# The head of a scan kernel: sums first, convolution by lines with two tiles in turn, first delta inside SBUF

## Chip, core and metric

The kernel runs on one NeuronCore of one Trainium2 chip. The metric is the device time of one execution in microseconds (us). TensorE is called PE, VectorE DVE, ScalarE ACT, GpSimd POOL, and SyncE SP; SP here issues most of the DMAs.

## What is computed

The input x is (4, 64, 64, 96) in f32: four images ("batches") of 4096 positions with 96 channels. Layer 0 is a binary hybrid of convolution and selective scan; layer 1 is an attention without softmax and a quantised feed-forward. Only layer 0 of the first batch is touched by the change:

```python
# x: (4, 64, 64, 96); Dn = 192, N = 16, R = 6, K = 4 directions, L = 4096
xz = bilinear(gn(x), W_in, s_in, b_in)          # sign(x - group mean) @ sign(W - mean).T, 384 wide
xp, z = split(xz, 2)
t = sign(xp + move0)
t = conv3x3(t, scale * sign(conv_W)) + conv_b   # 192 -> 192
t = prelu(t) + rp_b1 + xp
u = silu(t)                                     # (B, 192, 64, 64)
xs = [u by rows, u by columns, both reversed]   # K = 4
dts, Bs, Cs = split(bilinear(xs, Wl, sl, bl))   # R + 2 N rows ("rows" below)
delta = softplus(bilinear(dts, Wd, sd, bd) + dt_bias)
for each direction k, channel d, state n:       # along L
    h[l] = exp(delta[l] * A[n]) * h[l-1] + delta[l] * u[l] * B[n, l]
    y[l] += h[l] * C[n, l]
y = layernorm(y + D * u) * silu(z)              # then sign(...) into W_out
x = x + bilinear(y, W_out, s_out, b_out)
# ... layer 1: x + attention(ln(x)), x + ffn(ln(x))
```

## The kernel before

The scan is cut into 1536 pieces of 128 partitions by 1024 positions (32 channels times 4 states). Each takes an Exp on ACT ("decay"), a product delta·u·B on POOL ("inject"), a scan on DVE, a product with C on POOL or DVE, and a sum over states on PE. The pieces of one batch overlap with the other batches' remaining stages; what stands ahead of the first piece, for batch 0 alone, is called the head (`alone` is true there). `run` advances two generators in turn, the preparation of weights (`weights`) and the stages of batch 0 (`prologue`), until the rows of the first direction are there.

The loads of the constants inside `weights` (sbR: scale and bias of the rows; anm: the state matrix A):

```python
nc.gpsimd.memset(sbR, 0.0)
for k in range(NK):
    o, r0 = k % 2, 64 * (k // 2)
    nc.scalar.dma_start(sbR[r0 : r0 + 32, o, 0:1], a["sl_bc"][0:32, k : k + 1])
    nc.scalar.dma_start(sbR[r0 : r0 + 32, o, 1:2], a["bl_bc"][:, 32 * k : 32 * k + 32].rearrange("o p -> p o"))
    nc.scalar.dma_start(sbR[r0 + 32 : r0 + 32 + NR, o, :], a["sl_dt"][k])
for g in range(NG):
    src = a["al"][32 * (g % 4) : 32 * (g % 4) + 32, g // 4].rearrange("d k (q j) -> j d (k q)", j=4)
    for j in range(4):
        nc.sync.dma_start(anm[j::4, g, :], src[j])
for t in gTs + [wdz]:
    nc.gpsimd.memset(t.bitcast(F32), 0.0)

# ... [cut: mean and sign of W_in, its transposes]
# ... [cut: weight transposes through two PSUM banks with tags y0, y1 (`transposed`), reductions, casts]
```

The sums over x and the first sign of batch 0 (`c.later.store` puts a DMA into a list that `tick` issues on SP later; `bank(name, j)` gives one of the PSUM banks y0, y1):

```python
csum = bank("csum", 0)[0:1, 0 : 4 * DM]
for i in range(0, NT, 4):
    nc.tensor.matmul(
        csum, c.ones1, xts[i // 8][:, i % 8 : i % 8 + 4, :].rearrange("p i e -> p (i e)"),
        start=(i == 0), stop=(i == NT - 4),
    )
    if i % 8 == 4:
        yield
row = f32("csr")[0:1, 0 : 4 * DM]
nc.scalar.copy(row, csum)
# ... [cut: two small matmuls turn the row and add the groups]
negm = f32("negm")[0:96, 0:1]
nc.scalar.mul(negm, gsum, -1.0 / (3 * L))

def xfin(q, ps):
    cols = slice(512 * q, 512 * q + 512)
    nc.scalar.activation(xsT[:, cols], ps, AF.Sign, bias=negm, saturate=False)
    t = f32(f"xb{q}")[0:96]
    nc.scalar.activation(t, ps, AF.Identity, bias=c.bo)
    c.later.store(c.xbd[b][:, cols], t)

# ... [cut: transposes of x feed xfin, 8 tiles]
```

The projection of one part (h: half of the channels, q: eighth of the image) and the convolution:

```python
two = [c.p.dA.tile([128, CH], F32, name=f"cv{i}_{b}", tag="dA") for i in range(2)] if alone else None

def project(h, q):

    cols = slice(512 * q, 512 * q + 512)
    if alone:
        px, pz = two[1][:, 0:512], two[1][0:96, 512:CH]
    else:
        px, pz = bank(f"ix{h}{q}", 0), bank(f"iz{h}{q}", 1)[0:96]
    nc.tensor.matmul(px, c.winB if h else c.winT[:, 0:128], xsT[:, cols], start=True, stop=True)
    nc.tensor.matmul(
        pz, c.winT[:, DN + 96 * h : DN + 96 * h + 96], xsT[:, cols], start=True, stop=True
    )
    yield
    for rows, back in ((slice(0, 64), 0), (slice(64, 128), 1)) if h else ((slice(0, 128), 0),):
        nc.scalar.activation(
            tpad[h][rows, 1 + 8 * q : 9 + 8 * q, 1 - back : 1 - back + IW],
            px[rows].rearrange("p (h w) -> p h w", w=IW), AF.Sign,
            scale=c.pvx[rows, h, S_X : S_X + 1], bias=c.sbx[rows, h : h + 1], saturate=False,
        )
    sz = c.p.h.tile([128, CH], F32, name=f"sz{h}{q}_{b}", tag="h") if alone else f32(f"sz{h}{q}")
    sz = sz[0:96, 0:256].bitcast(BF16)
    nc.scalar.activation(
        sz, pz, AF.Sign, scale=pv[:, h, S_Z : S_Z + 1], bias=pv[:, h, B_Z : B_Z + 1]
    )
    c.later.store(c.szd[b][h][:, cols], sz)
# ... [cut: the first four projections ahead]
parts = [(h, q) for h in range(2) for q in range(NQ8)]
# ... [cut]
def by_columns(h, q, u):

    if q % 4 == 0:
        uts[h] = utp.tile([96, IW, 32], F32, name=f"ut{h}{q}_{b}", tag="ut")
    ut, at = uts[h], 8 * (q % 4)
    dst, src = ut[:, :, at : at + 8], u.rearrange("p (h w) -> p w h", w=IW)
    (nc.gpsimd.tensor_copy if alone else nc.scalar.copy)(dst, src)
    if q % 4 == 3:
        rows = slice(8 * q - 24, 8 * q + 8)
        c.later.store(c.utd[b][h].rearrange("p (w h) -> p w h", h=IH)[:, :, rows], ut, after=1)

# ... [cut: sign(h, q, pz) makes sg on ACT and stores it to xg in three pieces]
for n, part in enumerate(parts + [None]):
    if part:
        h, q = part
        nm = f"{h}{q}"
        at = 512 * (n % 2)
        ps = (two[0][:, at : at + 512] if alone else bank("cv" + nm, 0))[0:96]
    for s in range(4 if alone else 5):
        if part:
            per = 4 if alone else 3
            for tp, w, dy, dx in taps[per * s : per * s + per]:
                nc.tensor.matmul(
                    ps, w[:, 96 * h : 96 * h + 96], tp[:, 8 * q + dy : 8 * q + dy + 8, dx : dx + IW],
                    start=(w is taps[0][1]), stop=(w is taps[-1][1]),
                )
        if alone and ahead:
            if s % 2 == 0:
                next(ahead[0])
            else:
                next(ahead.pop(0), None)
        if prev:                    # [abridged to the case of alone]
            if s == 0:
                c.vec.scalar_tensor_tensor(pz, pz, pv[:, ph, S_X : S_X + 1], v, ALU.mult, ALU.add)
                c.vec.scalar_tensor_tensor(pz, r, c.oma[:, one(ph)], pz, ALU.mult, ALU.add)
            elif s == 1:
                sign(ph, pq, pz)
                nc.scalar.activation(e, pz, AF.Exp, scale=-1.0)
            elif s == 2:
                nc.scalar.activation(e, e, AF.Ln, bias=1.0)
                nc.scalar.activation(e, e, AF.Exp, scale=-1.0)
            elif s == 3:
                c.vec.tensor_tensor(u, pz, e, ALU.mult)
                c.later.store(c.ud[b][ph][:, 512 * pq : 512 * pq + 512], u)
                by_columns(ph, pq, u)
    if part:
        v, r = f32("v" + nm)[0:96], f32("r" + nm)[0:96]
        if alone:
            nc.vector.tensor_scalar(v, ps, c.acs[:, one(h)], c.acb[:, one(h)], ALU.mult, ALU.add)
        nc.scalar.activation(r, ps, AF.Relu, scale=c.csc[:, one(h)], bias=c.cbias[:, one(h)])
        pz = bank("cz" + nm, n % 2 if alone else 1)[0:96]
        nc.tensor.matmul(
            pz, c.winT[:, 96 * h : 96 * h + 96], xsT[:, 512 * q : 512 * q + 512], start=True, stop=True
        )
# ... [cut]
```

Then the rows: xr is turned from xg by PE and copied by ACT, the sums acc are scaled into tbc (B and C) and signed into sgn (dts):

```python
for o in (1, 0):
    xr = rw.tile([128, 96, 64], BF16, name=f"xr{o}_{b}", tag="xr")
    # ... [cut]
        if prev:
            nc.scalar.copy(prev[0], prev[1])
            prev = None
    # ... [cut]
                nc.scalar.activation(tbg[:, :, dv], sv, AF.Identity, scale=sc[0], bias=sc[1])
                nc.scalar.activation(sgg[:, :, dv], sv, AF.Sign, scale=sc[0], bias=sc[1], saturate=False)
# ... [cut]
```

Last, the first three parts of delta (`prepare`, ending in stores to dld in HBM), and the loop over pieces:

```python
def run(self, back):
    c, lanes, n = self.c, [], len(self.pieces)

    w = [c.p.w.tile([128, CH], F32, name=f"w_s{x}", tag="w") for x in range(8)]
    ps = [c.p.dA.tile([128, CH], F32, name=f"dA_s{x}", tag="dA") for x in range(2)]
    for x in range(3):
        half = slice(512 * (x % 2), 512 * (x % 2) + 512)
        lanes.append(
            self.prepare((
                w[x].rearrange("p (t l) -> p t l", t=2), w[3 + x // 2][:, half], w[5 + x // 2], ps[x // 2][:, half],
            ))
        )
    interleave(lanes)
    c.nc.scalar.activation(c.anm, c.anm, AF.Exp)
    c.nc.vector.tensor_scalar(c.anm, c.anm, -1.0, None, ALU.mult)
    for q in range(NQ):
        self.load_bc(0, self.bt, 0, 0, 0, q)
        self.load_bc(1, self.ct, 0, 0, 0, q)
    while lanes:
        interleave(lanes)
        c.later.tick()
    c.later.flush()
    self.load_dl(0)
    for m in (1, 2):
        self.load_dl(m)

    u = c.p.pu.tile([128, CH], F32, name="pu_s", tag="pu")
    for _ in self.prepare((w[7].rearrange("p (t l) -> p t l", t=2), w[4][:, 512:CH], u, ps[1][:, 512:CH])):
        pass
    self.decay(0)
    for i in range(AHEAD):
        self.inject(i)
    for i in range(n):
        self.at = i
        self.loads(i)
        # ... [cut: sums, carry, decay, reduce, inject, late product, scan of piece i]
```

Of the kernel before, what the change touches and what calls it, by code (L numbers as in the profile page):

```python
# [11 lines left out]
F32 = mybir.dt.float32  # L12
# [13 lines left out]
CH = 1024  # L26
# [27 lines left out]
def hybrid_kernel(ctx: ExitStack, tc: tile.TileContext, a: dict, out: bass.AP):  # L54
# [108 lines left out]
    def weights():  # L163
# [97 lines left out]
        for k in range(NK):  # L261
            o, r0 = k % 2, 64 * (k // 2)
            nc.scalar.dma_start(sbR[r0 : r0 + 32, o, 0:1], a["sl_bc"][0:32, k : k + 1])
            nc.scalar.dma_start(sbR[r0 : r0 + 32, o, 1:2], a["bl_bc"][:, 32 * k : 32 * k + 32].rearrange("o p -> p o"))
            nc.scalar.dma_start(sbR[r0 + 32 : r0 + 32 + NR, o, :], a["sl_dt"][k])
        for g in range(NG):
            src = a["al"][32 * (g % 4) : 32 * (g % 4) + 32, g // 4].rearrange("d k (q j) -> j d (k q)", j=4)
            for j in range(4):
                nc.sync.dma_start(anm[j::4, g, :], src[j])
        for t in gTs + [wdz]:  # L270
            nc.gpsimd.memset(t.bitcast(F32), 0.0)

# [113 lines left out]
        for name, dst in (("w1", w1q), ("w2", w2q), ("b1", b1q), ("b2", b2q)):  # L386
            q = dst if dst.dtype == F8 else temp(name + "q", list(dst.shape), F8)
            nc.vector.tensor_copy(q, small[name], saturate=False)
            if q is not dst:
                nc.vector.tensor_copy(dst, q)  # L390

# [58 lines left out]
def run(c):  # L450
# [6 lines left out]
    while (0, 1) not in c.ready:  # L457
        interleave(lanes)
        c.later.tick()
    scans = Scans(c)  # L460
# [39 lines left out]
def prologue(c, b, xts=None):  # L500
# [11 lines left out]
    with tc.tile_pool(name=f"xg_{b}", bufs=1) as xgp:  # L512
# [3 lines left out]
        with tc.tile_pool(name=f"cv_{b}", bufs=1) as cvp:  # L516
# [40 lines left out]
            def xfin(q, ps):  # L557
# [3 lines left out]
                nc.scalar.activation(t, ps, AF.Identity, bias=c.bo)  # L561
                c.later.store(c.xbd[b][:, cols], t)

            last = None
# [13 lines left out]
            two = [c.p.dA.tile([128, CH], F32, name=f"cv{i}_{b}", tag="dA") for i in range(2)] if alone else None  # L578

            def project(h, q):  # L580

                cols = slice(512 * q, 512 * q + 512)
                if alone:
                    px, pz = two[1][:, 0:512], two[1][0:96, 512:CH]
# [13 lines left out]
                sz = c.p.h.tile([128, CH], F32, name=f"sz{h}{q}_{b}", tag="h") if alone else f32(f"sz{h}{q}")  # L598
                sz = sz[0:96, 0:256].bitcast(BF16)
# [3 lines left out]
                c.later.store(c.szd[b][h][:, cols], sz)  # L603
# [16 lines left out]
            parts = [(h, q) for h in range(2) for q in range(NQ8)]  # L620
            taps = [(tpad[0], c.cwA[:, 3 * dy + dx], dy, dx) for dy in range(3) for dx in range(3)]
# [6 lines left out]
            def by_columns(h, q, u):  # L628

                if q % 4 == 0:  # L630
                    uts[h] = utp.tile([96, IW, 32], F32, name=f"ut{h}{q}_{b}", tag="ut")
                ut, at = uts[h], 8 * (q % 4)
                dst, src = ut[:, :, at : at + 8], u.rearrange("p (h w) -> p w h", w=IW)
                (nc.gpsimd.tensor_copy if alone else nc.scalar.copy)(dst, src)
                if q % 4 == 3:
                    rows = slice(8 * q - 24, 8 * q + 8)
# [12 lines left out]
            for n, part in enumerate(parts + [None]):  # L649
                if part:  # L650
                    h, q = part
                    nm = f"{h}{q}"
                    at = 512 * (n % 2)
                    ps = (two[0][:, at : at + 512] if alone else bank("cv" + nm, 0))[0:96]
                for s in range(4 if alone else 5):
# [7 lines left out]
                    if alone and ahead:  # L663
                        if s % 2 == 0:
                            next(ahead[0])
                        else:
# [53 lines left out]
        with tc.tile_pool(name=f"rw_{b}", bufs=1) as rw:  # L720

# [6 lines left out]
            for o in (1, 0):  # L728
                xr = rw.tile([128, 96, 64], BF16, name=f"xr{o}_{b}", tag="xr")
# [8 lines left out]
                for n in range(13):  # L738
                    if prev:
                        nc.scalar.copy(prev[0], prev[1])  # L740
# [17 lines left out]
                for gh in range(2):  # L758
                    groups = slice(32 * gh, 32 * gh + 32)
                    prev = None  # L760
                    for n in range(5):
                        if prev is not None:
# [3 lines left out]
                            nc.scalar.activation(tbg[:, :, dv], sv, AF.Identity, scale=sc[0], bias=sc[1])  # L766
# [429 lines left out]
class Scans:  # L1196
# [232 lines left out]

    def run(self, back):  # L1430
        c, lanes, n = self.c, [], len(self.pieces)

        w = [c.p.w.tile([128, CH], F32, name=f"w_s{x}", tag="w") for x in range(8)]
        ps = [c.p.dA.tile([128, CH], F32, name=f"dA_s{x}", tag="dA") for x in range(2)]
        for x in range(3):
            half = slice(512 * (x % 2), 512 * (x % 2) + 512)
            lanes.append(
                self.prepare((
# [133 lines left out]
```

## Time and profile before

| what | value |
| --- | --- |
| time, median of 3 runs | 5511.64 us (5508.68 to 5516.53) |
| span of the profiled execution | 5504.2 us |
| granted TensorE clock, mean | 0.717 |
| first sum over x on PE (csum) | 18.60 to 26.29 us |
| first and last r of the convolution on ACT | 81.56 and 188.53 us |
| first copy of xr on ACT | 202.85 us |
| first product on POOL | 260.93 us |
| first scan on DVE | 271.15 us |

The page of a profile gives, in its first part, the busy time of each engine with its share of the span; in its second, 40 equal slices of the span with the busy share in tenths. A line of the groups or of the timeline reads: (start,) busy time, engine, line of the kernel, operation, output<-input, shape, count, and in brackets the idle time before it with what ended it. A line of the waits reads: engine, line and tile that waited, what released it, microseconds in total, times, longest. A line of the stretches reads: from:to, length, then for PE, PEld (weight loads), DVE, ACT and POOL the busy time and the number of instructions, then the granted clock, the share in which the DMA engines were busy, and GB/s. Line 421 is a helper that issues the DVE and POOL operations, and line 440 issues the stores of the list; their groups are told apart by tile names.

### The profile page before, as it was taken

The numbers are of one execution on the slowest core, as the hardware profiler recorded it, in microseconds if no ns is written. First come the engines' busy times: TensorE is split into PE (matmuls) and PEld (weight loads), VectorE is DVE, ScalarE is ACT, GpSimd is POOL, SyncE is SP. The second block draws the span as 40 slices with busy tenths as digits, with TensorE's granted clock in tenths as the row PEclk, the third lists the DMA queues.
The fourth block names the chain that finished last, engine by engine and source line by source line (L and its number), as shares of the span: only waits on it lengthen the run. The fifth ranks groups of instructions, "written<-read, shape, count | busy, mean of one in ns | idle before, by whom it ended". The sixth has DMA issues, their size and how long they took to land. (4 is left out here: it accounts for less than half of the span.)

```text
span 5504.2 us, 62064 instructions
## 1 busy us (share of the span) xinstructions
PE 3466.0 (63%) x20089; PEld 1360.3 (25%) x20089; DVE 4996.1 (91%) x3142; ACT 3631.0 (66%) x5673; POOL 4947.3 (90%) x2247
## 2 busy tenths in 40 slices
PE   5456765467655776656665677664777664444677
PEld 2221222122222232222222222221232221111223
DVE  3299999999999999999999999999999999999884
ACT  4468776677766667777767666775656775655544
POOL 2199999899999999999999999999999999999981
PEclk7666876578867777768876787766787665556777
DMA  4455665766666666676765666666666565765642
GB/s 78 122 184 195 206 203 188 245 214 208 209 200 202 195 205 211 201 235 212 219 192 185 207 211 195 205 217 225 198 209 203 178 198 196 219 204 185 203 152 60
DMA packets 613659, 1069.84 MB, mean 194 GB/s; under 512 B 225147, under 2 KB 344468, under 8 KB 611540
## 3 DMA queue, kind: packets, MB, share of 16 engines
q1 hardware_dynamic: 612244, 1065.86, 61.3%
q8 instruction: 157, 2.57, 0.2%
q14 instruction: 170, 1.39, 0.1%
q10 hardware_dynamic: 1088, 0.02, 0.0%
HBM read 833.16 MB, written 229.35 MB: 193 GB/s over the span
## 5 line engine op out<-in xcount | busy, mean ns | idle before, releaser
L421 POOL TENSOR_TENSOR w<-dl,bc 128x1024 f32<-128x1024 f32 x1536 | 3580.9, 2358 | 155.5 <-PE yp L1409 72.6
L1336 ACT ACTIVATE dA<-dl,anm 128x1024 f32<-128x1024 f32 x1536 | 1714.5, 1116 | 474.4 <-DVE w L421 285.8
L421 DVE TENSOR_TENSOR_SCAN dA<-dA,cy,w 128x1024 f32<-128x1024 f32 x726 | 1700.9, 2343 | 90.7 <-ACT dA L1336 75.5
L1409 PE MATMUL yp<-w,sum 128*32 128x256 f32 x12288 | 1286.6, 514 | 384.8 <-POOL w L421 230.7
L421 POOL TENSOR_TENSOR w<-h,bc 128x1024 f32<-128x1024 f32 x573 | 1349.1, 2355 | 124.1 <-DVE h L421 110.0
L421 DVE TENSOR_TENSOR w<-dA,bc 128x1024 f32<-128x1024 f32 x963 | 1179.5, 1225 | 54.7 <-DVE dA L421 0.5
L421 DVE TENSOR_TENSOR_SCAN h<-dA,cy,w 128x1024 f32<-128x1024 f32 x426 | 996.7, 2340 | 16.0 <-ACT dA L1336 15.8
L1409 PEld LDWEIGHTS yp<-w,sum 128*32 128x32 f32 x12288 | 315.6, 128 | 1467.9 <-issue 690.1
L1378 ACT COPY cy<-dA 128x1 f32<-128x1 f32 x721 | 113.5, 157 | 772.5 <-DVE w L421 770.6
L421 DVE TENSOR_TENSOR_SCAN dA<-dA,w 128x1024 f32<-128x1024 f32 x237 | 540.9, 2282 | 36.7 <-ACT dA L1336 28.4
L1271 PE MATMUL dps<-gT,wdz 128*128 128x64 fp8e5 x1000 | 113.9, 313 | 358.8 <-ACT ys L1423 329.8
L421 DVE TENSOR_TENSOR_SCAN h<-dA,w 128x1024 f32<-128x1024 f32 x147 | 334.8, 2278 | 4.9 <-ACT dA L1336 3.4
L1284 PE MATMUL dps<-sp,ident 128*128 128x512 f32 x376 | 273.0, 815 | 46.0 <-ACT dps L1280 45.8
L1414 PE MATMUL yp<-ya,back 128*128 128x256 f32 x576 | 235.1, 528 | 4.5 <-DMA ya<-yd 2.5
L659 PE MATMUL cv<-tp,cwA 128*96 128x512 fp8e5 x576 | 198.4, 470 | 60.3 <-ACT r L706 55.1
L1271 PEld LDWEIGHTS <-wdz 128*128 128x128 fp8e5 x1024 | 95.4, 152 | 440.1 <-issue 409.7
L1271 PE MATMUL dps<-gT,wdy 128*128 128x64 fp8e5 x504 | 58.5, 317 | 205.2 <-ACT ys L1423 203.2
L1276 ACT ACTIVATE pd<-dps,dbias,pvd 128x512 f32<-128x512 f32 x188 | 143.3, 762 | 20.2 <-PE dps L1271 20.2
L1414 PEld LDWEIGHTS yp<-ya,back 128*128 128x128 f32 x576 | 122.6, 246 | 133.4 <-issue 93.5
L1378 ACT COPY cy<-h 128x1 f32<-128x1 f32 x431 | 79.9, 185 | 113.7 <-DVE h L421 112.8
L941 PE MATMUL yc<-eys,mean 96*96 96x512 f32 x240 | 132.1, 702 | 24.2 <-DVE vks L421 8.9
L1277 ACT ACTIVATE sp<-dps,dbias,pvd 128x512 f32<-128x512 f32 x188 | 144.2, 767 | 0.0
(312 smaller groups left out, 4433.1 us busy)
## 6 DMA issues: line engine op xcount, KB each, us to landing
dl<-dld SPq DMA_DIRECT2D x768, 512.0 KB
bc<-bcd SPq DMA_DIRECT2D x512, 512.0 KB
dld<-pd SPq DMA_DIRECT2D x125, 512.0 KB
yd<-ys SPq DMA_DIRECT2D x768, 64.0 KB
dld<-pd SPq DMA_DIRECT2D x126, 256.0 KB
ya<-yd SPq DMA_DIRECT2D x192, 128.0 KB
pu<-ud SPq DMA_DIRECT2D x32, 512.0 KB
pu<-utd SPq DMA_DIRECT2D x30, 512.0 KB
```

The lines of the kernel that those rows point to most:

```text
L421: return getattr(self.eng, name)(out, *args, **kw)
L659: nc.tensor.matmul(ps, w[:, 96 * h : 96 * h + 96], tp[:, 8 * q + dy : 8 * q + dy + 8, dx : dx + IW], start=(w is taps[0][1]), stop=(w is t ...
L941: self.c.nc.tensor.matmul(ps, w, x, start=(i == 0), stop=(i == len(pairs) - 1))
L1271: nc.tensor.matmul(pv[:, s], wd[:, k, s], gT[:, :, c0 : c0 + 16], start=(s == 0), stop=(s == 7))
L1276: nc.scalar.activation(d[:, 0], ps, AF.Abs, scale=sc, bias=bi)
L1277: nc.scalar.activation(t, ps, AF.Relu, scale=sc, bias=bi)
L1284: nc.tensor.matmul(ps, c.ident, t, start=False, stop=True, skip_group_check=True)
L1336: c.nc.scalar.activation(t, self.dlt[i // NQ][0], AF.Exp, scale=c.anm[:, g, NQ * KORD[e] + q : NQ * KORD[e] + q + 1])
L1378: self.c.nc.scalar.copy(self.carries[g, q], h[:, CH - 1 : CH])
L1409: c.nc.tensor.matmul(y[32 * x : 32 * x + 32, g % 2, :], c.sum4, prod[:, 256 * x : 256 * x + 256], start=(q == 0), stop=(q == NQ - 1 and no ...
L1414: c.nc.tensor.matmul(y[:, g % 2, :], w, src, start=False, stop=(n == len(more) - 1))
```

## The change

It concerns the head alone, and the start of the scan. (1) The sums over x are taken before the weights' transposes, xb moves from ACT to DVE, and the loads of sbR and anm move from the start to the end of `weights` and onto SP. (2) The projection uses one bank each of y0 and y1 instead of half a dA tile, one projection goes with each part of the convolution instead of two, and the z signs are collected four at a time. (3) The convolution takes both halves of the channels line by line, with a dA tile of its own for every part, so that PE can write one while the other is read. (4) The copies of xr alternate between DVE and ACT, and tbc goes to DVE. (5) The first delta is made in halves without the PE addition, and its copies to the 128-partition form go from SBUF to SBUF; the HBM copy is written afterwards.

```diff
         nc.gpsimd.memset(sbR, 0.0)
-        for k in range(NK):
-            o, r0 = k % 2, 64 * (k // 2)
-            nc.scalar.dma_start(sbR[r0 : r0 + 32, o, 0:1], a["sl_bc"][0:32, k : k + 1])
-            nc.scalar.dma_start(sbR[r0 : r0 + 32, o, 1:2], a["bl_bc"][:, 32 * k : 32 * k + 32].rearrange("o p -> p o"))
-            nc.scalar.dma_start(sbR[r0 + 32 : r0 + 32 + NR, o, :], a["sl_dt"][k])
-        for g in range(NG):
-            src = a["al"][32 * (g % 4) : 32 * (g % 4) + 32, g // 4].rearrange("d k (q j) -> j d (k q)", j=4)
-            for j in range(4):
-                nc.sync.dma_start(anm[j::4, g, :], src[j])
         for t in gTs + [wdz]:
             nc.gpsimd.memset(t.bitcast(F32), 0.0)
+        yield
 

 ... [cut: the same loads, now after the last weights, on nc.sync]
+                if alone:
+                    nc.vector.tensor_scalar(t, ps, c.bo, None, ALU.add)
+                else:
+                    nc.scalar.activation(t, ps, AF.Identity, bias=c.bo)
 ... [cut]
-            two = [c.p.dA.tile([128, CH], F32, name=f"cv{i}_{b}", tag="dA") for i in range(2)] if alone else None
+            szs = {}
 
             def project(h, q):
 
                 cols = slice(512 * q, 512 * q + 512)
                 if alone:
-                    px, pz = two[1][:, 0:512], two[1][0:96, 512:CH]
+                    px, pz = (
+                        c.p.ps.tile([128, 512], F32, name=f"i{x}{h}{q}_{b}", tag=f"y{j}") for j, x in enumerate("xz")
+                    )
+                    pz = pz[0:96]
                 else:
                     px, pz = bank(f"ix{h}{q}", 0), bank(f"iz{h}{q}", 1)[0:96]
 ... [cut]
+                if alone:
+
+                    if q % 4 == 0:
+                        szs[h] = c.p.w.tile([128, CH], F32, name=f"sz{h}{q}_{b}", tag="w")[0:96].bitcast(BF16)
+                    sz = szs[h][:, 512 * (q % 4) : 512 * (q % 4) + 512]
+                else:
+                    sz = f32(f"sz{h}{q}")[0:96, 0:256].bitcast(BF16)
                 nc.scalar.activation(
                     sz, pz, AF.Sign, scale=pv[:, h, S_Z : S_Z + 1], bias=pv[:, h, B_Z : B_Z + 1]
                 )
-                c.later.store(c.szd[b][h][:, cols], sz)
+                if not alone:
+                    c.later.store(c.szd[b][h][:, cols], sz)
+                elif q % 4 == 3:
+                    c.later.store(c.szd[b][h][:, 512 * q - 1536 : 512 * q + 512], szs[h])
 ... [cut]
+            if alone:
+                parts = [(h, q) for q in range(NQ8) for h in range(2)]
 ... [cut]
-                if q % 4 == 0:
-                    uts[h] = utp.tile([96, IW, 32], F32, name=f"ut{h}{q}_{b}", tag="ut")
-                ut, at = uts[h], 8 * (q % 4)
+
+                per = 2 if alone and h else 4
+                if q % per == 0:
+                    uts[h] = utp.tile([96, IW, 8 * per], F32, name=f"ut{h}{q}_{b}", tag=f"ut{h if alone else 0}")
+                ut, at = uts[h], 8 * (q % per)
 ... [cut]
-                    at = 512 * (n % 2)
-                    ps = (two[0][:, at : at + 512] if alone else bank("cv" + nm, 0))[0:96]
+                    if alone:
+                        ps = c.p.dA.tile([128, CH], F32, name=f"cv{nm}_{b}", tag="dA")[0:96, 0:512]
+                    else:
+                        ps = bank("cv" + nm, 0)[0:96]
                 for s in range(4 if alone else 5):
                     if part:
                         per = 4 if alone else 3
-                        if s % 2 == 0:
+                        if s == 0:
                             next(ahead[0])
-                        else:
+                        elif s == 2:
 ... [cut]
-                        nc.scalar.copy(prev[0], prev[1])
+                        (nc.vector.tensor_copy if fast and n % 2 else nc.scalar.copy)(prev[0], prev[1])
 ... [cut]
+                            if fast:
+                                nc.vector.tensor_scalar(tbg[:, :, dv], sv, sc[0], sc[1], ALU.mult, ALU.add)
+                            else:
+                                nc.scalar.activation(tbg[:, :, dv], sv, AF.Identity, scale=sc[0], bias=sc[1])
 ... [cut]
+    def start(self):
+
+        nc, c, p = self.c.nc, self.c, self.c.p
+        k, todo = KORD[0], [self.todo.pop(0) for _ in range(3)]
+        w = [p.w.tile([128, CH], F32, name=f"w_s{x}", tag="w") for x in range(8)]
+        t, d2, us = w[4:6], w[6], w[2:4]
+        ud = c.utd[0].rearrange("h p (n l) -> (h p) n l", l=IW)
+        v = [u.rearrange("p (n l) -> p n l", l=IW) for u in us]
+        nc.sync.dma_start(v[0], ud[0:128, 0:16])
+        for q in range(NQ):
+            self.load_bc(0, self.bt, 0, 0, 0, q)
+        for x in range(2):
+            nc.sync.dma_start(v[1][64 * x : 64 * x + 64, 0:8], ud[128:DN, 8 * x : 8 * x + 8])
+        self.next_part = self.prepare()
+        next(self.next_part)
+        gT = self.gs[0, k]
+        pss = [p.dA.tile([128, CH], F32, name=f"dA_s{x}", tag="dA")[:, 0:512] for x in range(2)]
+        pss.append(p.ps.tile([128, 512], F32, name="dps_s", tag="y0"))
 ... [cut]
+        def part(x):
+            ps, t, (d, du) = pss[x], ts[x], ds[x]
+            wd, c0 = (c.wdz, 16 * x) if x < 2 else (c.wdy, 0)
+            pv = ps.rearrange("p (c q s) -> p s q c", q=4, s=8)
+            for s in range(8):
+                nc.tensor.matmul(pv[:, s], wd[:, k, s], gT[:, :, c0 : c0 + 16], start=(s == 0), stop=(s == 7))
+            yield
+            sc, bi = c.pvd[:, x // 2, k : k + 1], c.dbias[:, x // 2, k : k + 1]
+            nc.scalar.activation(d, ps, AF.Abs, scale=sc, bias=bi)
+            nc.scalar.activation(t, ps, AF.Relu, scale=sc, bias=bi)
+            yield
+            nc.scalar.activation(d, d, AF.Exp, scale=-1.0)
+            yield
+            nc.scalar.activation(ps, d, AF.Ln, bias=1.0)
+            yield
+            c.vec.tensor_tensor(d, ps, t, ALU.add)
+            c.vec.tensor_tensor(du, d, uvs[x], ALU.mult)
+
+        lanes = [part(0), part(1)]
+        while lanes:
+            interleave(lanes)
+        nc.scalar.activation(c.anm, c.anm, AF.Exp)
+        nc.vector.tensor_scalar(c.anm, c.anm, -1.0, None, ALU.mult)
+        for n in range(3):
+            pair = []
+            for x in range(2):
+                r = p.dl.tile([128, CH], F32, name=f"dl{x}_s{n}", tag=f"dl{x}")
+                nc.sync.dma_start(r, w[x][32 * n : 32 * n + 32].unsqueeze(1).to_broadcast([32, 4, CH]))
+                pair.append(r)
+            self.dlt[n] = pair
+            if n == 0:
+                for q in range(NQ):
+                    self.load_bc(1, self.ct, 0, 0, 0, q)
 ... [cut: part 2, then d and du to HBM]
+        for _ in self.start():
             pass
         self.decay(0)
         for i in range(AHEAD):
             self.inject(i)
+
+        lanes.append(self.next_part)
         for i in range(n):
             self.at = i
             self.loads(i)
-            interleave(lanes)
+            for _ in range(3 if i < 3 else 1):
+                interleave(lanes)
```

## The prediction

> **What bounds the kernel now.** The page first: shares by engine, then the slices of 137.6 us (5504.2/40), since a share is an average over stages.
>
> ```profile
> PE 3466.0 (63%) x20089; PEld 1360.3 (25%) x20089; DVE 4996.1 (91%) x3142; ACT 3631.0 (66%) x5673; POOL 4947.3 (90%) x2247
> ...
> DVE  3299999999999999999999999999999999999884
> ...
> POOL 2199999899999999999999999999999999999981
> ```
>
> DVE and POOL are full from the third slice to the last three. Neither is full in the first two: the head, where batch 0 alone runs through input, projection, convolution, rows and first delta before the first scan. The scan loop after it holds the same 1536 scans and products before and after the change. So the change shifts the moment at which both full engines start, and the time moves by that shift. The table by stretches shows the moment: the columns are PE, PEld, DVE, ACT, POOL.
>
> ```profile
> 200.00:240.00 40.00, 18.71 (x184) 15.35 (x183) 0.21 (x1) 25.35 (x42) 0.21 (x2) 0.54 0.32 82
> 260.00:280.00 20.00, 3.64 (x28) 2.13 (x27) 8.05 (x5) 7.17 (x12) 19.07 (x9) 0.50 0.48 171
> 280.00:320.00 40.00, 21.98 (x196) 9.17 (x196) 39.55 (x24) 30.04 (x50) 40.00 (x18) 0.67 0.40 128
> ```
>
> POOL is full from 261 us, DVE from about 277. The waits of the first 280 us name the candidates:
>
> ```profile
> POOL w L421 <- DMA dl<-dld: 57.8, 1, 57.8
> PE cv L659 <- ACT r L706: 33.3, 15, 3.7
> DVE w_s L421 <- DMA pu_s<-utd: 22.3, 1, 22.3
> ACT r L706 <- DVE v L703: 21.2, 11, 2.9
> ACT slab L277 <- DMA sbR<-in_sl_dt: 15.3, 1, 15.3
> ACT sz L600 <- DMA szd<-sz: 12.2, 1, 12.2
> ACT xr L740 <- DMA utd<-ut: 10.2, 1, 10.2
> ```
>
> PE's 33.3 us look like the prize of the convolution, but ACT's wait for v two lines on says that ACT and VectorE go round a loop of their own. Two stretches of the timeline, ACT in the convolution, then the first delta:
>
> ```profile
> 134.04 0.77 ACT L706 ACTIVATE r<-cv,cbias,csc 96x512 f32<-96x512 f32 x1 [2.86 <-DVE v L703]
> 135.70 0.59 ACT L641 ACTIVATE sg<-cz 96x512 fp8e5<-96x512 f32 x1 [0.89 <-DVE cz L421]
> 139.63 0.78 ACT L706 ACTIVATE r<-cv,cbias,csc 96x512 f32<-96x512 f32 x1 [1.53 <-DVE v L703]
> ```
> ```profile
> 246.22 3.09 SPq L440 DMA_DIRECT2D dld<-w_s  x4
> 253.90 4.84 SPq L1313 DMA_DIRECT2D dl<-dld  x6
> 260.93 13.84 POOL L421 TENSOR_TENSOR w<-dl,bc 128x1024 f32<-128x1024 f32 x6 [57.84 <-DMA dl<-dld]
> 271.15 4.47 DVE L421 TENSOR_TENSOR_SCAN h<-dA,w 128x1024 f32<-128x1024 f32 x2 [1.74 <-ACT dA L1336]
> 277.11 2.29 DVE L421 TENSOR_TENSOR_SCAN h<-dA,w 128x1024 f32<-128x1024 f32 x1 [1.49 <-POOL w L421]
> ```
>
> The delta goes to HBM and back (issued 246.22, first product 260.93), and the third scan, 277.11, is held by POOL and no longer by the delta.
>
> **What the skill says.** "Perfetto Trace Analysis", Optimization Strategy: the most contended engine can differ by regime and should be judged inside the regime; the slices agree (3, 2 against 9). "DMA: Bandwidth & Descriptors", Issuing engines are not separate DMA queues: issue time is usually small beside the transfer. The trace differs: the 24 loads of anm, 2 KB each, hold the SP queue for 18.07 us. The same page, Where 436 GB/s comes from: copies inside SBUF are limited to 435 GB/s and those with HBM to about 358; between 236 and 252 us the DMA moved 297 to 407 GB/s, so I take 360; no run here shows an SBUF copy. "TensorE: Matmul & The Clock Gate", Wait — 56ns, not 53.3ns?: a 512-column matmul takes 427 ns with a cold array and 216 warm; the trace has both (four in 1.91 us, four in 1.04), so part of PE's time in the convolution is half clock.
>
> **Part by part.** *Sums.* csum runs at 18.60 to 26.29 because PE must do the transposes of winT first, which hang on an ACT sign (17.37) behind the sbR issues. Taken first, csum follows the loads of x: about 12.5, negm about 15.4 (30.56 before; same 4.3 us minus waits for ACT), xsT0 about 19 against 32.01. But xb goes to VectorE, behind the conv-weight reductions that end at 25.64, and the second transpose tile waits for xb. So I count 6 to 7 us, not 13. *Projection.* The z signs collect in a tile of their own: the 12.2 us stall is gone. But px and pz now share the two PSUM banks y0/y1 with the weight transposes, each emptied by a VectorE cast of 1.22 us or an ACT sign of 0.78: eight such takings ahead of the convolution at about 1.1 us hand back 8.7. First r: 81.56 − 12.2 − 6.5 + 8.7 = 71.5, gain 10.
>
> *Convolution.* Two tiles free PE from r (33.3 us). The loop that remains is r .77, handoff and cz .9, sg .49, e three times .62 to .66, u .7, v .8, then r again, which waits for v, and v stands behind u on VectorE: 5.65 us (139.63 to 145.27). A projection adds its ACT work: .68 + .68 for h=0 gives 7.0, 1.57 + .68 for h=1 gives 7.9. Fifteen intervals: 6 × 7.9 + 5 × 7.0 + 4 × 5.65 = 105. Before they took 188.53 − 81.56 = 107.0 (two projections per part for five, then none). The gain in PE's wait is thus 2 us. Against it: 2 us in the first interval, and 36 loads (12 sbR, 4.5 us; anm, 18.07) that now stand on SP behind the first part's stores, about 75.6 to 100. A later part's sg store waits behind them and its tile is reused: I take 6.5 us (0 to 10). So r of the last part is at 71.5 + 105 + 8.5 = 185.0, u at 189.2 (192.73 before).
>
> *By lines, utd.* Both halves now finish together, so two transposed stores end the stage; the second issues some 2.8 us later than the single one. Before, 10.1 us passed from u's start to the landing (202.85); I take 12.9: 202.1. The xr copies wait for all of utd in both kernels. 3.5 us shrink to 0.8.
>
> *Rows.* The copies alternate between ACT and VectorE, but each bank's cycle is a matmul of .54, a copy of .6 and two handoffs, 1.3 us per pair against 1.26. tbc on VectorE precedes the sign of the same tile on ACT, which waits for it: 1.43 per tile against 1.34. Zero.
>
> *First delta.* gT ends at 231.1 (clock of before). Then 8 more matmuls (1.0) ahead, first Abs 233.9, four Abs/Relu at .67, two Exp at .65, two Ln at .6: Ln ends 239.2; add and product on VectorE at .69: d at 240.9, du at 241.5. Copies of dl go at once, behind 3.4 MB (u, bc, u), which at 360 GB/s take 9.4 us from 233.5; they add 1 MB, 2.9 us: landed about 248. First product 248.2 against 260.93: 12.7 gained on POOL. VectorE: scan 0 is at 250.6 against 271.15, but scan 2 waits for POOL's late product behind six first ones (6 × 2.31 + 2.35, 264.6) and scan 3 for the next late one, one more product and a late one after it: 248.2 + 13.84 + 3 × 2.35 = 269.3 against 279.32. So VectorE gains 10.0, not 20.
>
> Sum: 0.8 + 10.0 to 12.7; I count 10.2, as VectorE is the fuller of the two. 5511.6 − 11 = 5500.6, stated as 5500.
>
> **Rivals.** *All gains add:* 13 from sums, 12 stall, 33 from PE's wait, 20 first scan, the gaps being real: −40 to −70, 5440 to 5470. For: DVE has 13 of 40 us work on average in the head, so there is room. Against: ACT's wait for v, and scan 2 waiting for POOL. *Queue and stores take it back:* the 22.6 us of SP issue fall where 3 stores per part must leave, and the two last utd stores stand before the rows: head +5 to +10 beyond my count, result 5503 to 5512. For: SP was blocked 6.03 us behind one utd store (195.27). *Absorbed in the loop:* the dl and bc loads of the next groups come later than the scans that start early, so scans idle and the 10 shrink to 3: 5508. For: 171 GB/s only at 260 to 280, so room; against it too, thus weak. *Faster rows:* if the xr copies truly alternate, −2.
>
> **Range and chances.** Three runs span 7.9 us, so the base alone is good to 3 us. The head terms have errors of about 5 (projection), 4 (queue), 3 (stores), 3 (landing): root of the squares 8. The first rival's long arm makes the low side wider. 5486 to 5509. Two per cent is 110 us, a good third of the head: no mechanism here reaches it.
>
> **What would show it.** In the changed profile: no stall of the sz sign; r of the first part near 71, of the last near 185, period 5.65 in parts without projection with "r <- v" in the waits; the 24 anm issues in the middle of the convolution and a wait of e or sg for xg; xr still waiting for utd until about 202; first POOL product near 248, first scan near 250, scan 3 near 269. It is wrong if r comes every 4.5 us or less, if xr starts before 197 or after 207, or if the scan loop with equal counts takes another time from the first full stretch to the end.

## The result and the profile after

The changed kernel takes 5499.6 us (median of 4 runs, 5497.7 to 5501.9) against 5512.5 us for the kernel before in the same comparison: ratio 0.9977, 95% interval 0.9959 to 0.9994. A later comparison with more runs gives 5499.9 (14 runs) against 5510.8 (18 runs), ratio 0.9979 (0.9971 to 0.9987). The change makes the kernel some 11 us faster, 0.2%.

The page of the changed kernel, engine shares and two rows of slices:

```profile
PE 3473.7 (63%) x20083; PEld 1362.6 (25%) x20083; DVE 5013.3 (91%) x3167; ACT 3616.0 (66%) x5648; POOL 4947.1 (90%) x2247
...
DVE  4499999999999999999999999999999999999984
...
POOL 2399999899999999999999999999999999999981
```

DVE's first two slices went from 3, 2 to 4, 4 and POOL's second from 1 to 3; both engines fill up earlier and stay full as before. The waits of the first 280 us; all but the fourth answer to lines shown of before:

```profile
POOL w L423 <- DMA bc<-bcd: 46.6, 1, 46.6
...
ACT r L728 <- DVE v L725: 29.4, 16, 4.3
...
ACT xr L764 <- DMA utd<-ut: 12.3, 1, 12.3
...
PE xps L573 <- DVE xb L565: 10.3, 3, 9.6
...
PE cv L681 <- ACT r L728: 5.2, 9, 1.2
```

PE's wait for r fell from 33.3 to 5.2 us, but ACT's wait for v rose from 21.2 to 29.4 and now stands before every one of the 16 parts. The stalls for sbR and szd are gone. A new one is PE's 9.6 us for xb. xr still waits for utd. POOL's first product now ends its wait with B (bc); of the ten other runs with the new start, three end it with B and seven with the copies of the delta (dl_s), so the two land close together. The end of the convolution on ACT, three lines of the timeline:

```profile
167.01 0.78 ACT L728 ACTIVATE r<-cv,cbias,csc 96x512 f32<-96x512 f32 x1 [1.47 <-DVE v L725]
168.72 0.59 ACT L661 ACTIVATE sg<-cz 96x512 fp8e5<-96x512 f32 x1 [0.94 <-DVE cz L423]
...
172.65 0.77 ACT L728 ACTIVATE r<-cv,cbias,csc 96x512 f32<-96x512 f32 x1 [1.53 <-DVE v L725]
```

From r to r it is 5.64 us, with the same two gaps as before (for cz, for v). And the start of the loop, over SP, POOL and DVE:

```profile
226.61 1.41 SPq L1508 DMA_DIRECT2D dl_s<-w_s  x2
...
228.07 7.40 SPq L1329 DMA_DIRECT2D bc<-bcd  x4
...
236.03 9.26 POOL L423 TENSOR_TENSOR w<-dl_s,bc 128x1024 f32<-128x1024 f32 x4 [46.63 <-DMA bc<-bcd]
...
238.40 4.60 DVE L423 TENSOR_TENSOR_SCAN h<-dA,w 128x1024 f32<-128x1024 f32 x2 [5.18 <-POOL w L423]
...
246.52 4.64 POOL L423 TENSOR_TENSOR w<-dl_s,bc 128x1024 f32<-128x1024 f32 x2 [1.23 <-DMA dl_s<-w_s]
...
253.49 2.29 DVE L423 TENSOR_TENSOR_SCAN h<-dA,w 128x1024 f32<-128x1024 f32 x1 [9.91 <-POOL w L423]
...
259.44 2.29 DVE L423 TENSOR_TENSOR_SCAN h<-dA,w 128x1024 f32<-128x1024 f32 x1 [3.67 <-POOL w L423]
```

The first scan is 32.8 us earlier than before (238.40 against 271.15), but scans 2 and 3 wait 9.91 and 3.67 us for POOL, and piece 3 is 19.9 us earlier (259.44 against 279.32). The marks side by side, in us; "again" is a second execution that was profiled later, and the loop is the span less the start of piece 3:

| mark | before | before, again | after | after, again | predicted |
| --- | --- | --- | --- | --- | --- |
| last sign of x | 47.2 | 46.2 | 40.6 | 39.4 | 6 to 7 earlier |
| first r | 81.6 | 80.5 | 64.8 | 64.0 | 71.5 |
| last r | 188.5 | 184.3 | 172.7 | 171.8 | 185.0 |
| first xr | 202.9 | 198.6 | 189.1 | 188.3 | 202.1 |
| signs gT end | 231.1 | 226.9 | 217.4 | 216.7 | some 230.3 |
| first product | 260.9 | 256.7 | 236.0 | 235.2 | 248.2 |
| piece 3 | 279.3 | 275.0 | 259.4 | 259.4 | 269.3 |
| loop | 5224.9 | 5237.1 | 5236.5 | 5240.6 | equal |

So the time came out as predicted while the way to it did not: the head gained 13.7 us up to the signs (0.8 in the sum), all of it ahead of the convolution (16.7 us at the first r, 15.9 at the last; the fifteen intervals from first to last r take 107.8 us, before 107.0 and 103.7), the first delta a further 6.2 (10.0 in the sum), and of the 19.9 us together (17.8 against the mean of the two profiles of before) only 11 reached the end. The experiments ask where each of these came from.

### The profile page after: what moved, and what is told of

It reads as the page before. It is cut to its first block, busy times and chain, and to the rows that moved or that the text cites. A ratio compares the mean times of both kernels' runs of the same rounds, so it can differ in the third digit from the quotient of the medians.

```text
span 5495.9 us, 62028 instructions
## 1 busy us (share of the span) xinstructions
PE 3473.7 (63%) x20083; PEld 1362.6 (25%) x20083; DVE 5013.3 (91%) x3167; ACT 3616.0 (66%) x5648; POOL 4947.1 (90%) x2247
```

## The experiments

Times are medians over repeated runs, compared with runs of the kernel before on the same chip. The experiment with one tile, the second execution of the kernel before and the three runs on single terms have one execution each and are read by their marks alone: their times, 5494.9 to 5513.9 us, tell little, since the lowest belongs to the run with early loads, whose head is 2 us worse than that of the changed kernel.

### The two halves apart

The changed kernel with the old start (parts 1 to 4 of the change), and the kernel before with the new start (part 5):

```diff
-    def start(self): ...          # first delta from SBUF to SBUF
+    # run() of the kernel before: prepare() into spare tiles, dld in HBM, load_dl
```

> The changed kernel with the first delta as before (through HBM, four parts prepared ahead of the first piece); sums, convolution, projection and rows stay changed. The signs of the first direction should end at 217.4 us as in the changed kernel (231.1 before) and the scan of piece 3 should start at about 265.6 (279.3 - 13.7). Theory A (the end moves with the scan of piece 3, the length of the loop differs only by chance): 5512.5 - 13.7 = 5499. Theory B (the loop is longer because of the new start): also about 5499, with a loop of the length of before, 5225 us from piece 3 to the end. Theory C (an earlier head is partly given back by the loop whatever the start): loop 5230 to 5236, time 5503 to 5508.

> The kernel before with only the first delta and the start of the loop changed (copies from SBUF to SBUF). Signs end at 231.1 as before; first product at about 249.8 (18.7 after the signs), scan of piece 3 at about 273 (279.3 - 6.2). Theory A: time 5512.5 - 6 = 5506. Theory B: the new start costs the loop 8 to 12 us, so the time is 5512 to 5517, no better than before. Theory C: 5508 or so.

The old start took 5501.1 us (18 runs; before 5510.9; ratio 0.9984, 0.9977 to 0.9991): signs at 216.9, piece 3 at 264.4. The new start alone took 5509.0 (13 runs; ratio 0.9995, 0.9987 to 1.0003): first product at 248.5, piece 3 at 272.6. The halves add up within their intervals: 9.8 + 1.9 = 11.7 us, the whole 11. The head carries nearly all of it. The new start, 4.6 us earlier at piece 3 than the mean of the two profiles of before (277.2), is worth 1.9 us, not distinguishable from nothing.

The loops by the median (time less the start of piece 3; a time is some 2 us more than its span) are 5236.7 and 5236.4. Theory B as written fell: the loop with the old start is not at 5225, and the new start alone did not take 5512 to 5517. The old start lies between A (5499) and C (5503 to 5508), the new start nearer to C (5508) than to A (5506). The loop of before that all three were measured against, 5225, proves too short in the second profile of that kernel, below.

A small part of theory B is in the traces all the same. From piece 3 to piece 40 the kernel before takes 117.9 us in both profiles and the old start 117.6, but the new start alone takes 119.7 and the changed kernel 119.9 in both profiles. VectorE is busy for the same 114.3 to 114.4 us in each of these stretches. Every later run with the new start lies at 119.7 to 119.9 too. So the new start gives back 2 us over these 37 pieces, every time.

### The loop of ACT and VectorE in the convolution

v of the next part, and its first cz, go ahead of u on VectorE:

```diff
+                    if alone and part and s == 3:
+                        nc.vector.tensor_scalar(nv, ps, c.acs[:, one(h)], c.acb[:, one(h)], ALU.mult, ALU.add)
+                        nc.tensor.matmul(npz, c.winT[...], xsT[...], start=True, stop=True)
+                        c.vec.scalar_tensor_tensor(npz, npz, pv[:, h, S_X : S_X + 1], nv, ALU.mult, ALU.add)
                     if prev:                      # s == 3: u of the part before
```

> The changed kernel with the loop r, cz, sg, e, u, v, r cut: v of the next part, and its first cz, are put ahead of u on VectorE. If the loop of ACT and VectorE sets the period of the convolution, it falls from 5.65 to about 4.15 us without projection and from 6.8 / 7.7 to 5.4 / 6.3 with one; the last r moves from 172.7 to about 152 and everything after it by 20: time 5480 (theory A), or 5485 to 5490 if the loop gives back a part (C). Rival: PE sets the period as soon as ACT and VectorE let go (15 matmuls of 0.213 us at full clock, 0.427 at half clock, so 3.9 to 7.8 us a part): last r at 165 or later, time 5492 or more.

The time fell to 5477.2 us (5 runs; ratio 0.9939, 0.9925 to 0.9952), 22 to 23 us below the changed kernel. The timeline of ACT in this kernel:

```profile
139.37 0.76 ACT L730 ACTIVATE r<-cv,cbias,csc 96x512 f32<-96x512 f32 x1
140.95 0.59 ACT L661 ACTIVATE sg<-cz 96x512 fp8e5<-96x512 f32 x1 [0.82 <-DVE cz L423]
...
143.25 0.76 ACT L730 ACTIVATE r<-cv,cbias,csc 96x512 f32<-96x512 f32 x1
```

The gap for v is gone and the period is 3.9 us (expected 4.15); with a projection it is mostly 5.1 and 6.0. What is left of the period is ACT's own work, 3.06 us, and 0.82 us for cz. The last r is at 151.6, 21 us earlier, as theory A had it. PE's rival period of up to 7.8 us doesn't appear. It was the loop r, cz, sg, e, u, v that set the pace, and the wait "r <- v" named it before the change was run.

The opposite edit, one PSUM tile for all parts so that PE must wait for r again:

```diff
-                        ps = c.p.dA.tile([128, CH], F32, name=f"cv{nm}_{b}", tag="dA")[0:96, 0:512]
+                        ps = cvt        # one tile, taken once before the loop
```

> The changed kernel with one PSUM tile for all parts of the convolution, so that PE waits for r again. By the prediction's loop (r, cz, sg, e, u, v) PE's wait is hidden: r to the end of the next 15 matmuls at full clock is .9 + 3.4 + .4 and v .9, 5.6 us, as long as the loop itself; periods 5.6 to 6.8 without projection, 7 to 8 with, last r at 174 to 180 instead of 172.7. If the second tile is what shortened the convolution, its 33 us of PE wait return: last r at 190 or later.

```profile
PE cv L683 <- ACT r L730: 35.4, 14, 3.7
ACT r L730 <- DVE v L727: 32.3, 16, 4.3
```

PE's wait is back in full, 35.4 us, and the last r moves to 175.3 only (fifteen intervals of 111.3 us instead of 107.8): 30 us of wait are worth 3 us. The line numbers are those of that kernel.

### xr and the transposed stores

xr gets a pool of its own, so that its copies don't wait for the stores of the transposed tiles (to utd), although by the sizes in the kernel it need not overlap them (xr has 12,288 bytes a partition, and xsT and the two padded inputs, laid out ahead of the transposed tiles, have 12,808; the traces show no addresses); and the last store of the first half goes behind the last signs:

```diff
-        with tc.tile_pool(name=f"rw_{b}", bufs=1) as rw:
-            xrs = rw.tile([128, 96, 64], BF16, name=f"xr_{b}", tag="xr")
+        with tc.tile_pool(name=f"rx_{b}", bufs=1) as rx, tc.tile_pool(name=f"rw_{b}", bufs=1) as rw:
+            xrs = rx.tile([128, 96, 64], BF16, name=f"xr_{b}", tag="xr")
...
-                    c.later.store(..., ut, after=1)
+                    c.later.store(..., ut, after=7 if alone and q == 7 and h == 0 else 1)
```

> The changed kernel with xr in a pool of its own, so that its copies no longer wait for the transposed stores, and with the last store of the first half put behind the last signs. The first copy of xr should come at about 178.5 instead of 189.1. tbc, still in the memory of the transposed tiles, then waits for those stores, which land at about 190; the rows gain about 8, first product at 228: time 5492 (theory A). Rival: the wait only moves from xr to tbc and the whole gain is lost: rows end within 2 us of 212, time 5498 to 5500.

The head did as expected: first xr at 177.1, and tbc took over a part of the wait:

```profile
DVE tbc L791 <- DMA utd<-ut: 5.7, 1, 5.7
```

Signs at 210.1, 7.3 us earlier (the pool and the late store were not tried apart); first product at 228.9. But the time fell to 5475.8 us (5 runs; ratio 0.9936, 0.9924 to 0.9949), 24 us below the changed kernel, three times what the head explains. The rest had to be in the loop, where the later batches run the same stage. So the pool was split in the three later batches alone, with the head of the changed kernel:

> The changed kernel with xr in a pool of its own in the three later batches only; batch 0 as changed. Head as in the changed kernel (signs end at 217.4, piece 3 at 259.4). If ACT's waits for the transposed stores inside the loop (27.3 us in three waits) stall the decays and so the scans, the loop from piece 3 to the end falls from about 5240 to 5224 (as in the run with the pool in all batches) and the time to about 5486. Rival: the short loop of that run was chance (loops of one kernel differ by some us from execution to execution), and the time stays at 5496 to 5502.

5477.3 us (5 runs; ratio 0.9937, 0.9924 to 0.9951): 22 us less than the changed kernel with its head unchanged (signs 216.3, piece 3 at 259.5), and 9 less than expected. The profiled execution was the slowest of the five, 5487.3; its loop is 5226.0 (5224 expected), 10 to 15 below the two of the changed kernel. In the run before, 24.1 less the 7.2 of piece 3 leaves 17 us for the same pools. So their worth in the loop lies between 10 and 22 us; the intervals, 7 us to each side, do not fix it closer. What happens there in the changed kernel, once per batch, over ACT, DVE and POOL:

```profile
810.62 0.59 ACT L764 CAST xr<-xa 128x512 bf16<-128x512 f32 x1 [10.89 <-DMA utd<-ut]
```
```profile
812.52 2.35 DVE L423 TENSOR_TENSOR_SCAN h<-dA,cy,w 128x1024 f32<-128x1024 f32 x1 [7.41 <-ACT dA L1363]
```
```profile
814.95 2.37 POOL L423 TENSOR_TENSOR w<-h,bc 128x1024 f32<-128x1024 f32 x1 [6.85 <-DVE h L423]
```

A copy of the next batch stands in ACT's order and waits 10.89 us for a store; the decay of the current piece stands behind it, the scan waits for the decay (7.41 us) and POOL for the scan (6.85). Both engines that are otherwise full stand still. Three such waits add up to 27.3 us, here in the waits of the loop (300 to 5380 us), of after and then of before:

```profile
ACT xr L764 <- DMA utd<-ut: 27.3, 3, 10.9
```
```profile
ACT xr L740 <- DMA utd<-ut: 23.5, 3, 9.3
```

The second executions show 26.7 and 23.9; with the pool of its own the line is gone. The rival, that the short loop was chance, fell.

Both edits together:

> Both edits that helped, together: v ahead of u, and xr in a pool of its own in all batches with the last transposed store late. If the head's gains add and reach the end one for one: 5475.8 - 20 to 22 = 5454 to 5456, piece 3 at about 232. Rival: the transposed stores, each of 6144 pieces, now come in a shorter convolution and the wait moves to tbc; then 5460 to 5465.

5456.4 us (4 runs; ratio 0.9899, 0.9886 to 0.9913), 43 us below the changed kernel and 54 below the kernel before; piece 3 at 233.0, signs at 190.2. This is the fastest version of the study. The gains of the two edits (22.7 and 24.1) nearly add.

### How much a loop differs by itself

> The changed kernel once more, unchanged, for its own spread: time 5497 to 5503; the marks of the head within 1 us of the first profile (signs 217.4, first product 236.0, piece 3 at 259.4). The loop from piece 3 to the end, 5236.5 in the first profile, is open: within 2 us if it is a property of the kernel, 5 or more apart if it is chance.

> The kernel before once more, for a second look at its loop. The first profile has 5224.9 us from piece 3 to the end, but its execution was 5 us faster than the median of before; the median less the start of piece 3 gives 5231.5. Chance: the second loop is at 5229 to 5235, and the changed kernel's loops (5236.5, 5240.6) are 5 to 9 longer, not 12 to 16. Property: 5225 again.

The head of the changed kernel repeats within 1.2 us at every mark up to the first product, and piece 3 to 0.1. Its loop is 5236.5 and 5240.6, 4.1 apart and so between the two bounds set beforehand. The runs with the old start and with the pools of the later batches share this head up to the signs, which end there at 216.9 and 216.3 (217.4 and 216.7 here). The head of the kernel before doesn't repeat: last r at 188.5 and 184.3, signs at 231.1 and 226.9, piece 3 at 279.3 and 275.0; the new start alone shares it up to the signs and lies between, with signs at 229.9. From first to last r the three take 107.0, 103.7 and 105.3 us. The granted clock of PE in the three stretches from 80 to 190 us was 0.82, 0.88 and 0.89 in the first, 0.84, 0.91 and 0.92 in the second, and 0.83, 0.92 and 0.89 in the third. That fits a head in which PE is in the chain when its clock is low, but it is not shown: the clock was not varied on purpose. The loop of before is 5224.9 and 5237.1, further apart than either guess had it, so the first profile, from which the prediction was made, had a slow head and a short loop. By the medians, and the mean starts of piece 3, the loops are 5510.81 − 277.18 = 5233.6 before and 5499.86 − 259.43 = 5240.4 after: 6.8 us longer, where the first pair of profiles says 11.6. Of these, 2.0 us are lost between piece 3 and piece 40, with the new start. About 3 us more may be the longer waits of xr (27.0 against 23.7 on average); that is argued, not shown. What remains, 1 to 2 us, is well within what two executions of one kernel differ by.

### The single terms of the head

> The changed kernel with the z signs stored one by one from the two h tiles, as before, while the loads of sbR and anm stay behind the convolution's first part. The prediction gave 12.2 us to the collecting of the signs. If collecting is what removed ACT's stall, the stall comes back: first r at about 76. Rival: the stall was made by the 24 loads of anm on the same queue (43 to 61 us before), which now come later; then first r stays at 64 to 66 and collecting is worth 0 to 2.

```diff
-                    sz = szs[h][:, 512 * (q % 4) : 512 * (q % 4) + 512]      # four at a time, in w tiles
+                sz = c.p.h.tile(...)[0:96, 0:256].bitcast(BF16)              # one by one, in the two h tiles
```

First r at 63.2: the stall does not come back where it was. It comes back later, in the convolution, as one line of the waits up to 100 us:

```profile
ACT sz L608 <- DMA szd<-sz: 7.2, 1, 7.2
```

One interval of r is 14.9 us instead of 7.7, and the last r is at 178.3, 6 us later. In SP's queue the loads of anm begin at 75.12 and hold it for 16.25 us; the store that frees the tile of the signs leaves behind them, at 91.47. The kernel before has the same order in its queue ahead of its stall, which ended at 68.71:

```profile
43.03 18.07 SPq L269 DMA_DIRECT2D anm<-in_al  x24
61.21 4.49 SPq L440 DMA_DIRECT2D xbd<-xb  x8
65.80 14.37 SPq L440 DMA_DIRECT2D szd<-sz  x6
```

So the 24 loads of anm made most of the stall before, with the stores of xb behind them, and they make this one now that they stand in the convolution. The collecting matters because the loads moved there.

> The changed kernel with the loads of sbR and anm on SP at their old place in the program, ahead of the first weights; signs still collected. The prediction charged 6.5 us of the convolution to the 36 loads standing in its middle. If they cost anything there, the first interval of r falls from 12.1 to 8 and the last r from 172.7 to about 168. Rival (from the profile, in which VectorE's u of the first part stands behind operations of the weights): the first interval stays at 11 to 12.5 and the last r within 1.5 us of 172, unless the early loads now delay the stores of x and with them the head.

With the loads of sbR and anm early on SP, the intervals of r hardly change (first 11.7 instead of 12.1, then 6.8 and 7.8; all fifteen 107.0 instead of 107.8), so in the changed kernel they cost the convolution less than 1 us. Early, they hold back the stores of xb, and v waits for those (the waits, up to 100 us):

```profile
DVE v L724 <- DMA xbd<-xb: 4.1, 1, 4.1
```

First r at 67.2, signs at 219.0: 2 us worse. Moving the loads is worth 2 us with the collecting.

> The changed kernel with the sums over x behind the transposes of the input weights again. negm then at about 22 to 24 instead of 14.3. If sums first is worth its 6 to 7 us, the last sign of x and the first r come 6 us later (46 and 71). Rival: PE waits anyway for xb, which stands on VectorE behind the reductions of the convolution weights (24.8 us in the changed kernel), so the last sign of x stays within 1 us of 40 and the first r at 64 to 66; the gain at that place then comes from the loads that left ACT's queue.

negm at 24.6; last sign of x at 43.3, first r at 70.7, signs at 221.4. The sums first are worth 3 to 4 us at the last sign, 6 to 7 at the first r and 4 to 5 at the signs. The flat rival (nothing, because PE waits for xb anyway) fell; so did the full 6 us at the last sign of x, of which xb on VectorE keeps a part. The kernel before has negm at 30.6 and the last sign at 47.2, so the rest of the gain there, 3 to 4 us, comes from what this run keeps of the change: the loads off ACT's queue and xb off ACT, which were not tried apart.

## Why the prediction came out

The mechanism of the whole, "the scan loop holds the same work, so the end moves by the shift of the head", held in part: the two halves add (11.7 against 11.0), and a faster head reaches the end (v first: piece 3 is 18.1 us earlier, the time 22.7 less), but of the 17.8 us at piece 3 the loop gave back 7. That the size, 11 us, came out is luck: misses in the sum cancelled. Its last line does not add up either: 0.8 + 10.0 is 10.8, where it counts 10.2 and takes off 11. Step by step:

- *Sums.* Predicted negm 15.4, xsT 19, a gain of 6 to 7 held down by xb behind the reductions. Measured 14.3, 18.2 and 6.6; PE's 9.6 us wait for xb is in the profile. The sizes are right, but the order of the sums makes only 3 to 4 of the 6.6 us at the last sign of x.
- *Projection.* "eight such takings ahead of the convolution at about 1.1 us hand back 8.7" failed. From the last sign of x to the first r it was 34.3 us before and is 24.2 now, so of the stall's 12.2 only about 2 came back. Why so little came back was not tried; the casts of the weights were in the way before as well. First r 64.8 instead of 71.5: the term was 6.7 too large. And the stall was put down to the collecting alone; it was made by what stood in SP's queue, above all the loads of anm.
- *Convolution.* The loop and its periods held: 6.8 and 7.7 with a projection (7.0, 7.9), 5.6 to 6.0 without (5.65), and the gain by PE's freedom was small, 3 us in the one-tile run. The first interval was 12.1 where 9.9 stood: u of the first part starts at 74.00, after VectorE's small operations on weights. "I take 6.5 us (0 to 10)" for the loads in the middle failed: less than 1. The store behind them was indeed late (signs of the second part issued at 93.58), but nothing waited for it. Fifteen intervals took 107.8 instead of 113.5, and so no less than before (107.0 and 103.7).
- *utd.* From u to the first xr 12.2 us against 12.9; the wait of xr for utd was right.
- *Rows.* xr to the signs takes 28.3 us in both kernels: no gain from sharing with VectorE, as worked out; the rival *faster rows* fell with it.
- *First delta.* First product 18.6 us after the signs (17.1 predicted): it waited for B, which lands close to the copies. Behind the first two copies the issue of C stood 7.40 us, so the next copies left at 235.52 and POOL waited 1.23 for one of them. Piece 3 is 42.0 us after the signs (38.2 predicted, 48.2 before). The gain is 6.2 where 10.0 stood; the mechanism, that VectorE gains far less than its first scan because POOL's late products hold scans 2 and 3, held.
- *Equal loop.* Not in the sum as a term, and it gave back 7 us. This is the rival *absorbed in the loop*, which expected 10 us to shrink to 3 at the loads of the next groups. Early in the loop it took only 2.0 us: piece 3 is 19.9 us earlier and piece 40 still 17.9. Some 3 us may be longer waits of xr, the rest is open; where in the later loop they go differs between the two pairs of profiles.

Of the rivals, *all gains add* fell with the one-tile run: PE's 33 us were hidden. *Queue and stores take it back* fell with the early loads. The prediction's own test, "it is wrong if xr starts before 197", was met: xr starts at 189. *All gains add* also rested on a reading that is too high: its "13 of 40 us" of VectorE in the head are 11.6 over the seven stretches of 40 us up to 280. As an account of the gain it was therefore too low by 11 to 13 us in the head up to the signs, and too high by 4 in the first delta and by 7 in the loop.

## What to carry to other kernels

A long wait of one engine (PE for r, 33 us) says little when two others go round in a loop; the wait inside that loop (r for v, 21 us) is the one to cut, here by putting the next part's independent operation ahead in VectorE's order. In an interleaved loop, search for waits of an in-order engine that belong to another stage's work: three of them, 27 us in all and half a per cent of the span, cost some 22 us of the median time, and a pool of its own for the waiting tile took them away. Before dividing a small gain between its parts, profile the same kernel twice: here the head of one kernel moved by 4 us and its loop by 12.

## What the runs showed unexpectedly

- The head of the kernel before differs by 4 us between two executions, while that of the changed kernel repeats to about 1 us.
- The new start gives back 2 us between piece 3 and piece 40: 119.7 to 119.9 us in all eleven profiles with it, 117.6 to 117.9 in the three without, at the same busy time of VectorE.
- SP's four issues of C took 7.40 us in the changed kernel (7.40 to 7.96 in the eleven runs with the new start), where eight issues of B and C together took 5.82 before; what held them was not tried.
- 36 small loads in the middle of the convolution, 22 us of SP's queue, cost less than 1 us when no tile's reuse waits for the stores behind them, and 7.2 us when one does.
